# Selective scan of a vision mixer: two 512-column scans per state made one 1024-column scan, with the carried state added to the scan's input

## Chip, cores and metric

The kernel runs on one core of a Trainium2 chip. The metric is the device time in microseconds of the whole program, which computes a chain of network layers in one launch. The change touches the first layer only. Five engines work side by side: TensorE (PE, matmuls), VectorE (DVE), ScalarE (ACT), GpSimd (POOL) and SyncE (SP, which here only issues transfers). [...]

## The reference

The input is x of 2 x 64 x 64 x 128. Layer 0 normalises it, projects it to 256 channels, applies a depthwise 3 x 3 convolution and SiLU, and then runs a selective scan over the 4096 positions in four orders (K = 4: windows row by row, windows column by column, and both backwards). Cut to what matters:

```
delta = softplus(delta + delta_bias)
def step(h, inp):                      # h: 256 channels x 16 states, per order
    ut, dt, bt, ct = inp
    dA = exp(dt[..., None] * A4)       # A4 = -exp(A_logs)
    h = dA * h + (dt * ut)[..., None] * bt[:, :, None, :]
    y = einsum('bkdn,bkn->bkd', h, ct)
    return (h, y)
_, ys = lax.scan(step, zeros, xs_t)
y = ys + u * D
```

The four results are added, normalised over the channels, multiplied with SiLU(z) and projected back to 128 channels. Layers 1 (a deformable convolution), 2 (a larger selective scan and a spectral filter) and 3 (linear attention and experts) follow, each on the whole result of the one before.

## The kernel before

The 256 channels are two halves (h = 0, 1) of 128 partitions. For each of the two batch entries, and each of the four orders in the sequence kk = 0, 2, 1, 3, the 4096 positions are cut into eight **chunks** of T = 512 columns (ci = 0 to 7). Orders 2 and 3 run backwards: the access pattern of the scan is reversed, and the chunks come last to first. There are 2 x 4 x 8 = 64 chunks, and in each 16 **steps**, one for each state n.

A step does the following.

- POOL: S = du * B_n for both halves (L342, 1024 columns). du is dt times u, B_n a row spread over the partitions by a transfer into br. S has four buffers.
- ACT: dA = exp(dt * A_n) for each half (L345, 512 columns, in PSUM, four buffers of 512 columns).
- DVE: one scan for each half (L347), in place in S: S = dA * previous + S. Its initial value is 0 in the first chunk of an order and stt otherwise, the state kept from the chunk before.
- ACT: copies the last column of both halves into stt (L349), except in the last chunk.
- DVE: M = S * C_n for both halves (L361). C_n is spread over the partitions by a matmul into pcn (L316, one buffer).
- PE: adds M to yp through a multiplication by the identity (L376).

The section of steps is written under a manual schedule, so every engine's order is the order of the text. In each step the copy into stt is issued after the exponentials of that step but belongs to the step before. At step 0 the result of the chunk before is added into Y: by DVE for kk = 2 (L329) and for odd kk (L323), by a copy on ACT for kk = 0 (L327). Then u times D opens the new yp (L358).

The **prologue** of the next chunk (its u in scan order, the projections, softplus and du) is a generator, and each step of the current chunk advances it by one stage (`next(steps, None)`, behind M). Softplus is relu(v) + log(1 + e) with e = exp(-|v|), and the rounding of 1 + e is corrected by e - (u - 1), where u = 1 + e. By stage:

- 0 and 1: uc, the chunk's u, copied on ACT (L249, L253); 2: the projection px (PE, L257)
- 3: xd and its bf16 cast cs (ACT, L260, L265), xd's rows to DRAM, the matmul pd for half 0
- 4: r = xd - cs on POOL (L279), |v| and relu(v) of half 0 (ACT, L280, L281), pd for half 1; 5: |v| and relu(v) of half 1
- 6: two casts of r (ACT, L283, L284), e = exp (ACT, L285); 7: the third part of r (POOL, L287), u = 1 + e (ACT, L288)
- 8: dt += e (POOL, L290), a cast (ACT, L291), the logarithm into e (ACT, L292); it needs another function table, and the next dA needs the table of exp again
- 9: u - 1 (POOL, L294); 10: e - u (POOL, L296); 11: dt += e (POOL, L298); 12: du = dt * uc (POOL, L300)

Layer 2 of the same kernel, which the change leaves alone, already carries its state in the way that the change brings to layer 0: its scan starts from 0 in every chunk, and POOL multiplies the state by the first column's exponential (L1069) and adds it to the first column of S (L1070) behind the product that fills S (L1064).

Of the kernel before, what the change touches and what calls it, by code (L numbers as in the profile page):

```python
# [16 lines left out]
F32 = mybir.dt.float32  # L17
I32 = mybir.dt.int32
BF16 = mybir.dt.bfloat16
AF = mybir.ActivationFunctionType  # L20
ALU = mybir.AluOpType
AX = mybir.AxisListType
PSUM = bass.MemoryType.PSUM
DRAM = bass.MemoryType.DRAM

P = 128
# [132 lines left out]
def layer0(k):  # L159
    tc, nc, ins, X = k.tc, k.nc, k.ins, k.X  # L160
    T = N
    NC = L // T
    with ExitStack() as es:
# [18 lines left out]
        an = cst.tile([P, 8, 16], F32, name="an")  # L182
# [10 lines left out]
        for b in range(B):  # L193
# [36 lines left out]
            with ExitStack() as e2:  # L230
                ch = e2.enter_context(tc.tile_pool(name=f"l0h{b}", bufs=2))
# [2 lines left out]
                bcp = e2.enter_context(tc.tile_pool(name=f"l0e{b}", bufs=2, space=DRAM))  # L234
                ps = e2.enter_context(tc.tile_pool(name=f"l0ys{b}", bufs=1, space=PSUM))
                pc_ = e2.enter_context(tc.tile_pool(name=f"l0yc{b}", bufs=1, space=PSUM))
                pa = e2.enter_context(tc.tile_pool(name=f"l0ya{b}", bufs=4, space=PSUM))
                py = e2.enter_context(tc.tile_pool(name=f"l0yp{b}", bufs=1, space=PSUM))
                stt = sm.tile([P, 16, 2], F32, name="stt")

                def prologue(kk, c, got):


                    uc = ch.tile([P, 2, T], F32, name="uc")
                    for h in range(2):
                        if kk % 2:
                            src = U[:, h, :].rearrange("p (g i w j) -> p w g j i", g=4, i=16, w=4)[:, c // 2, 2 * (c % 2) : 2 * (c % 2) + 2]
                            for g in range(2):
                                nc.scalar.copy(uc[:, h, g * 256 : (g + 1) * 256].rearrange("p (j i) -> p j i", j=16), src[:, g])  # L249
                        else:  # L250
                            src = U[:, h, (c // 2) * 1024 : (c // 2 + 1) * 1024].rearrange("p (i w j) -> p w i j", i=16, w=4)
                            for g in range(2):
                                nc.scalar.copy(uc[:, h, g * 256 : (g + 1) * 256].rearrange("p (i j) -> p i j", i=16), src[:, 2 * (c % 2) + g])  # L253
                        yield
                    px = ps.tile([P, N], F32, name="pd", tag="ps")
                    for h in range(2):
                        nc.tensor.matmul(px, w_xp[:, h, kk, :], uc[:, h, :], start=h == 0, stop=h == 1)  # L257
                    yield
                    xd = ch.tile([P, T], F32, name="xd")
                    nc.scalar.copy(xd, px)  # L260
                    bc = bcp.tile([16, T], F32, name="bc")
                    nc.sync.dma_start(out=bc, in_=xd[112:128, :])

                    cs = ch.tile([80, T], BF16, name="cs")
                    nc.scalar.copy(cs, xd[:80])  # L265


                    dt = ch.tile([P, 2, T], F32, name="dt")
                    du = ch.tile([P, 2, T], F32, name="du")
                    e = sm.tile([P, 2, T], F32, name="e")  # L270
                    u = sm.tile([P, 2, T], F32, name="u")
                    for h in range(2):
                        bias = k.v("dt_b")[:, kk * 2 + h : kk * 2 + h + 1]
                        pd = ps.tile([P, N], F32, name="pd", tag="ps")
                        nc.tensor.matmul(pd, w_dt[96:104, kk, h * P : (h + 1) * P], xd[96:104, :], start=True, stop=True)
                        yield
                        if h == 0:
                            r = sm.tile([80, T], F32, name="r")
                            nc.gpsimd.tensor_tensor(r, xd[:80], cs, ALU.subtract)  # L279
                        nc.scalar.activation(e[:, h, :], pd, AF.Abs, bias=bias)  # L280
                        nc.scalar.activation(dt[:, h, :], pd, AF.Relu, bias=bias)  # L281
                    yield
                    nc.scalar.copy(cs[32:64], r[32:64])  # L283
                    nc.scalar.copy(cs[64:80], r[64:80])  # L284
                    nc.scalar.activation(e, e, AF.Exp, scale=-1.0)  # L285
                    yield
                    nc.gpsimd.tensor_tensor(r[64:80], r[64:80], cs[64:80], ALU.subtract)  # L287
                    nc.scalar.activation(u, e, AF.Identity, bias=1.0)  # L288
                    yield
                    nc.gpsimd.tensor_tensor(dt, dt, e, ALU.add)  # L290
                    nc.scalar.copy(cs[64:80], r[64:80])  # L291
                    nc.scalar.activation(e, u, AF.Ln)  # L292
                    yield
                    nc.gpsimd.tensor_scalar(u, u, -1.0, None, ALU.add)  # L294
                    yield
                    nc.gpsimd.tensor_tensor(e, e, u, ALU.subtract)  # L296
                    yield
                    nc.gpsimd.tensor_tensor(dt, dt, e, ALU.add)  # L298
                    yield
                    nc.gpsimd.tensor_tensor(du, dt, uc, ALU.mult)  # L300
                    got.append((uc, bc, cs, dt, du))

                todo = [(kk, ci) for kk in (0, 2, 1, 3) for ci in range(NC)]
                at = lambda i: (todo[i][0], NC - 1 - todo[i][1] if todo[i][0] >= 2 else todo[i][1])
                ready = []
# [25 lines left out]
                with tc.manual_schedule():  # L331
                    rows, pcn, last, save = spread(ready[0][1], 0), c_row(ready[0][2], 0), None, None
                    for it, (kk, ci) in enumerate(todo):
                        c = at(it)[1]
                        uc, bc, cs, dt, du = ready.pop()
                        steps = prologue(*at(it + 1), ready) if it + 1 < len(todo) else iter(())
                        s_ = slice(None, None, -1) if kk >= 2 else slice(None)
                        for n in range(16):
                            if n % 4 == 0:
                                br = rows  # L340
                            S = wk.tile([P, 2, T], F32, name="S", bufs=4)
                            nc.gpsimd.tensor_tensor(S, du, br[:, n % 4, :].unsqueeze(1).to_broadcast([P, 2, T]), ALU.mult)  # L342
                            for h in range(2):
                                dA = pa.tile([P, T], F32, name="dA")
                                nc.scalar.activation(dA, dt[:, h, :], AF.Exp, scale=an[:, kk * 2 + h, n : n + 1])  # L345
                                init = 0.0 if ci == 0 else stt[:, n, h : h + 1]
                                nc.vector.tensor_tensor_scan(S[:, h, s_], dA[:, s_], S[:, h, s_], init, ALU.mult, ALU.add)  # L347
                            if save is not None:
                                nc.scalar.copy(*save)  # L349
                                save = None  # L350
                            if ci < NC - 1:
                                save = stt[:, n, :], (S[:, :, 0] if kk >= 2 else S[:, :, T - 1])
                            if n == 0:
                                if last is not None:
                                    add_up(*last)
                                yp = py.tile([P, 2, T], F32, name="yp")
                                for h in range(2):
                                    nc.tensor.matmul(yp[:, h, :], dd[:, kk * 2 + h, :], uc[:, h, :], start=True, stop=False)  # L358
                                last = kk, c, yp
                            M = wk.tile([P, 2, T], F32, name="M")  # L360
                            nc.vector.tensor_tensor(M, S, pcn.unsqueeze(1).to_broadcast([P, 2, T]), ALU.mult)  # L361
                            next(steps, None)
                            if n == 14:
                                for _ in steps:
                                    pass
                            if n < 15:
                                pcn = c_row(cs, n + 1)
                            elif ready:
                                pcn = c_row(ready[0][2], 0)
                            if n % 4 == 2:  # L370
                                if n < 14:
                                    rows = spread(bc, n // 4 + 1)
                                elif ready:
                                    rows = spread(ready[0][1], 0)
                            for h in range(2):
                                nc.tensor.matmul(yp[:, h, :], k.ident, M[:, h, :], start=False, stop=n == 15)  # L376
                    add_up(*last)
# [1111 lines left out]
```

## Time and profile before

| what | value |
|---|---|
| median of 3 runs | 16227.84 us (16219.87 to 16235.26) |
| profiled execution: its own time, span | 16221.3 us, 16219.5 us |
| busy DVE, POOL, PE, ACT over the span | 13938.5, 13438.3, 12269.0, 9683.1 us |
| layer 0, first and last scan (L347) | start at 250.4 and 4630.4 us |
| POOL idle before r (L279), in 64 chunks | 798.2 us |
| ACT table loads at L292 and L345 | 64 of each, 1283 ns |
| POOL u - 1 (L294), ACT 1 + e (L288) | 2769 ns, 1051 ns |

The span runs from the first to the last instruction. Busy time of an engine over the whole span says little here: layer 2's scan (L1120, 8192 instructions) alone is 9225.0 us of DVE. What the change is worth has to be read between about 250 and 4630 us. In a row of the page, "us, ns" after the bar are the group's busy time and the mean of one instruction; then comes the idle time of the engine just before these instructions, and who ended it.

### The profile page before, as it was taken

What the parts mean: (1) busy time and instruction counts of PE and PEld (TensorE: products, weight loads), DVE (VectorE), ACT (ScalarE), POOL (GpSimd) and SP (SyncE); (2) the same over time, 40 slices, a digit from 0 to 9 for tenths busy, and PEclk for the clock granted to TensorE, in tenths of its full rate; (3) what the DMA queues carried; (4) which work ended last, traced back from release to release, by engine and by line L of the source; (5) the groups of instructions that cost most, each with busy time, mean ns of one, the idle gap of its engine ahead of it and who ended that gap; (6) DMA issues with size and microseconds to landing.
All of it is one profiled execution on the core that took longest, in us unless ns stands there. A gap on an engine that the chain in (4) does not pass through costs nothing.

```text
span 16219.5 us, 191958 instructions
## 1 busy us (share of the span) xinstructions
PE 12269.0 (76%) x69886; PEld 7241.8 (45%) x69886; DVE 13938.5 (86%) x13011; ACT 9683.1 (60%) x15720; POOL 13438.3 (83%) x4181
## 2 busy tenths in 40 slices
PE   6666657666657874548688688888888888888897
PEld 2222223222225861215455355555545555555565
DVE  4999985999974349999999999999999999999973
ACT  3555534555520017777777677777777777777752
POOL 3888744888735879999999999999999999999970
PEclk8999989999988886769899799999999999999998
DMA  2111111111125544546565555655666666665553
GB/s 101 68 68 66 66 48 52 68 68 66 66 73 162 161 146 151 164 153 198 180 195 193 171 187 192 195 190 196 189 199 195 192 204 196 188 205 195 187 173 128
DMA packets 1214866, 2389.74 MB, mean 147 GB/s; under 512 B 346648, under 2 KB 923288, under 8 KB 1047904
## 3 DMA queue, kind: packets, MB, share of 16 engines
q1 hardware_dynamic: 1162672, 2206.74, 41.5%
q0 software_dynamic: 50384, 169.42, 3.5%
q8 instruction: 552, 9.04, 0.2%
q14 instruction: 394, 3.23, 0.1%
q10 hardware_dynamic: 864, 1.32, 0.0%
HBM read 2018.49 MB, written 358.65 MB: 147 GB/s over the span
## 4 chain that ended last, share of the span: by engine, by line
POOL 39%; DVE 18%; PE 15%; issue 5%; ACT 3%; DMA 3%; another core or an unknown queue 1%; SPq 0%; POOLq 0%; DVEq 0%; ACTq 0%
POOL S L1064 33%; DVE S L1120 11%; PE pef L948 6%; DVE S L347 5%; POOL G L516 2%; PE Z L1082 2%; DMA row<-drow 2%; PE acc L921 2%; POOL S L342 2%; PE pv L535 1%; PE pw L747 1%; PE po L468 1%; POOL S L1070 1%; DVE M L361 1%
## 5 line engine op out<-in xcount | busy, mean ns | idle before, releaser
L1120 DVE TENSOR_TENSOR_SCAN S<-dA,S 128x512 f32<-128x512 f32 x8192 | 9225.0, 1200 | 391.1 <-ACT dA L1118 209.4
L1064 POOL TENSOR_TENSOR S<-row,g 128x4096 f32<-128x4096 f32 x1024 | 9102.1, 8896 | 251.8 <-DMA row<-drow 191.1
L1118 ACT ACTIVATE dA<-row,a_t 128x512 f32<-128x512 f32 x8192 | 5615.4, 692 | 2148.0 <-DVE S L1120 2111.3
L1082 PE MATMUL Z<-S,cv 128*32 128x256 f32 x32768 | 2503.1, 435 | 1481.5 <-ACT ze L1088 1225.6
L948 PE MATMUL pef<-hk,ur 128*128 128x256 f32 x14336 | 3515.4, 388 | 135.4 <-ACT e L928 119.9
L948 PEld LDWEIGHTS pef<-hk,ur 128*128 128x128 f32 x14336 | 2647.1, 191 | 1076.7 <-issue 565.5
L342 POOL TENSOR_TENSOR S<-du,br 128x1024 f32<-128x1024 f32 x1024 | 2389.7, 2355 | 204.8 <-issue 109.2
L347 DVE TENSOR_TENSOR_SCAN S<-dA,stt,S 128x512 f32<-128x512 f32 x1792 | 2198.3, 1268 | 127.7 <-POOL S L342 95.5
L1082 PEld LDWEIGHTS Z<-S,cv 128*32 128x32 f32 x32768 | 1000.8, 121 | 2690.6 <-issue 1283.4
L376 PE MATMUL yp<-M,ident 128*128 128x512 f32 x4096 | 2091.7, 635 | 3.2 <-DVE M L361 3.2
L376 PEld LDWEIGHTS yp<-M,ident 128*128 128x128 f32 x4096 | 821.5, 201 | 2180.2 <-issue 2141.7
L345 ACT ACTIVATE dA<-dt,an 128x512 f32<-128x512 f32 x2048 | 1332.3, 680 | 187.5 <-DVE S L347 173.3
L316 PE MATMUL pcn<-cs,sel 80*128 80x512 bf16 x1024 | 405.6, 396 | 1261.6 <-DVE M L361 1212.4
L361 DVE TENSOR_TENSOR M<-S,pcn 128x1024 f32<-128x1024 f32 x1024 | 1250.6, 1221 | 108.2 <-PE pcn L316 4.8
L1088 ACT COPY ze<-Z 128x512 f32<-128x512 f32 x1024 | 1122.9, 1097 | 234.1 <-PE Z L1082 200.2
L921 PE MATMUL acc<-e,mw 128*128 128x512 f32 x1920 | 1043.5, 631 | 31.7 <-ACT e L928 31.1
L516 POOL DMA_INDIRECT G<-table,idx x576 | 797.1, 1384 | 261.1 <-issue 175.1
L349 ACT COPY stt<-S 128x2 f32<-128x2 f32 x896 | 170.8, 191 | 1376.3 <-DVE S L347 1365.7
L948 PEld LDWEIGHTS pef<-hd,ur 128*128 128x128 f32 x4096 | 758.1, 194 | 493.9 <-issue 235.4
L948 PE MATMUL pef<-hd,ur 128*128 128x256 f32 (+1 forms) x4096 | 876.7, 340 | 103.2 <-ACT e L928 97.2
L523 DVE TENSOR_TENSOR V<-G,wt 128x4608 f32<-128x4608 f32 x64 | 317.6, 4962 | 603.3 <-DMA G<-table,idx 594.8
L279 POOL TENSOR_TENSOR r<-xd,cs 80x512 f32<-80x512 f32 x64 | 73.8, 1152 | 798.2 <-ACT cs L265 798.2
(319 smaller groups left out, 9010.1 us busy)
## 6 DMA issues: line engine op xcount, KB each, us to landing
row<-drow SPq DMA_DIRECT2D x1024, 1024.0 KB
br<-bc SPq DMA_DIRECT2D x256, 1024.0 KB
zd<-ze SPq DMA_DIRECT2D x1024, 256.0 KB
hk<-in_phi_dram SPq DMA_DIRECT2D x128, 576.5 KB
hk<-in_phi_dram SPq DMA_DIRECT2D x96, 704.5 KB
hd<-in_phi_dram SPq DMA_DIRECT2D x512, 128.5 KB
mw<-wdr SPq DMA_DIRECT2D x480, 128.0 KB
hk<-in_phi_dram SPq DMA_DIRECT2D x160, 320.5 KB
```

What stands on the lines that cost most here:

```text
L342: nc.gpsimd.tensor_tensor(S, du, br[:, n % 4, :].unsqueeze(1).to_broadcast([P, 2, T]), ALU.mult)
L345: nc.scalar.activation(dA, dt[:, h, :], AF.Exp, scale=an[:, kk * 2 + h, n : n + 1])
L347: nc.vector.tensor_tensor_scan(S[:, h, s_], dA[:, s_], S[:, h, s_], init, ALU.mult, ALU.add)
L361: nc.vector.tensor_tensor(M, S, pcn.unsqueeze(1).to_broadcast([P, 2, T]), ALU.mult)
L376: nc.tensor.matmul(yp[:, h, :], k.ident, M[:, h, :], start=False, stop=n == 15)
L921: nc.tensor.matmul(acc.rearrange("p a s -> p (a s)"), ms[f][:, o, :], e, start=box["first"], stop="whole" in box and (f, o) == todo[-1])
L948: nc.tensor.matmul(pe[:, a, 256 - n :], ur[:, par, j, :], h[:, at : at + n], start=i == 0, stop=i + 1 == len(mm))
L1064: nc.gpsimd.tensor_tensor(S, row.unsqueeze(1).to_broadcast([P, 2, R, T]), g.unsqueeze(2).to_broadcast([P, 2, R, T]), ALU.mult)
L1082: nc.tensor.matmul(Z[32 * j : 32 * j + 32, q], cv[:, h, s], S[:, h, :, s], start=h == 0, stop=h == 1)
L1088: nc.scalar.copy(ze.rearrange("p q t e -> p q e t"), Z)
L1118: nc.scalar.activation(dA, row[:, j % R, :], AF.Exp, scale=a_t[:, h, d : d + 1])
L1120: nc.vector.tensor_tensor_scan(s, dA, s, 0.0, ALU.mult, ALU.add)
```

## The change

The two scans of a step become one over 2 x 512 columns, half 0 behind half 1 or the other way round, with initial value 0 throughout. So that one half doesn't run into the other, the exponential of each half's first column in scan order (f: column 0, or 511 backwards) is 0 in dA, set once for each order, and ACT writes only the other 511 columns. What the initial value did is now added to the input: POOL multiplies the kept state by ea, the exponential at column f for all 16 states, and adds it to column f of S. dA becomes two fixed buffers of 2 x 512 columns in place of four of 512. ea is computed by ACT at the end of the prologue. In the prologue u - 1 moves from POOL to ACT, and r is issued one stage later, at 5 in place of 4.

```
-  pa = ... tile_pool(name=f"l0ya{b}", bufs=4, space=PSUM)
+  pa = ... tile_pool(name=f"l0ya{b}", bufs=1, space=PSUM)
+  dAs = [pa.tile([P, 2, T], F32, name=f"dA{i}") for i in range(2)]
...
-                        if h == 0:
+                        if h == 1:
                             r = sm.tile([80, T], F32, name="r")
...
-                    nc.gpsimd.tensor_scalar(u, u, -1.0, None, ALU.add)
+                    nc.scalar.activation(u, u, AF.Identity, bias=-1.0)
...
-                    got.append((uc, bc, cs, dt, du))
+                    ea = ch.tile([P, 16, 2], F32, name="ea")
+                    f = T - 1 if kk >= 2 else 0
+                    for h in range(2):
+                        nc.scalar.activation(ea[:, :, h], an[:, kk * 2 + h, :], AF.Exp, scale=dt[:, h, f : f + 1])
+                    got.append((uc, bc, cs, dt, du, ea))
...
-                        uc, bc, cs, dt, du = ready.pop()
+                        uc, bc, cs, dt, du, ea = ready.pop()
+                        f = T - 1 if kk >= 2 else 0
+                        rest = slice(0, T - 1) if kk >= 2 else slice(1, T)
+                        if ci == 0:
+                            for t in dAs:
+                                nc.vector.memset(t[:, :, f : f + 1], 0.0)
...
                             nc.gpsimd.tensor_tensor(S, du, br[:, n % 4, :]..., ALU.mult)
+                            if ci > 0:
+                                if n in (0, 2):
+                                    m = slice(0, 14) if n == 0 else slice(14, 16)
+                                    nc.gpsimd.tensor_tensor(stt[:, m], stt[:, m], ea[:, m], ALU.mult)
+                                nc.gpsimd.tensor_tensor(S[:, :, f], S[:, :, f], stt[:, n, :], ALU.add)
+                            dA = dAs[n % 2]
                             for h in range(2):
-                                dA = pa.tile([P, T], F32, name="dA")
-                                nc.scalar.activation(dA, dt[:, h, :], AF.Exp, scale=an[:, kk * 2 + h, n : n + 1])
-                                init = 0.0 if ci == 0 else stt[:, n, h : h + 1]
-                                nc.vector.tensor_tensor_scan(S[:, h, s_], dA[:, s_], S[:, h, s_], init, ALU.mult, ALU.add)
+                                nc.scalar.activation(dA[:, h, rest], dt[:, h, rest], AF.Exp, scale=an[:, kk * 2 + h, n : n + 1])
+                            flat, dflat = (t.rearrange("p h t -> p (h t)")[:, s_] for t in (S, dA))
+                            nc.vector.tensor_tensor_scan(flat, dflat, flat, 0.0, ALU.mult, ALU.add)
```

More of the change, by code (lines that the diff above doesn't have):

```diff
@@ L236, in layer0 @@
                 pc_ = e2.enter_context(tc.tile_pool(name=f"l0yc{b}", bufs=1, space=PSUM))
-                pa = e2.enter_context(tc.tile_pool(name=f"l0ya{b}", bufs=4, space=PSUM))
+                pa = e2.enter_context(tc.tile_pool(name=f"l0ya{b}", bufs=1, space=PSUM))
                 py = e2.enter_context(tc.tile_pool(name=f"l0yp{b}", bufs=1, space=PSUM))
                 stt = sm.tile([P, 16, 2], F32, name="stt")
+                dAs = [pa.tile([P, 2, T], F32, name=f"dA{i}") for i in range(2)]
                 def prologue(kk, c, got):
```

## The prediction

> **What bounds the kernel now.** I read the busy times by stretch first, to see which engine is full while layer 0 runs; then the costliest groups, for the durations; then the timeline of one chunk, instruction by instruction, because a mean hides where the engines wait for each other. The table of stretches (after the length: busy and count of PE, PEld, DVE, ACT, POOL; then clock, DMA share, GB/s):
>
> ```profile
> 800.00:1200.00 400.00, 268.36 (x590) 104.88 (x589) 376.10 (x321) 217.08 (x414) 324.39 (x145) 0.94 0.18 66
> ```
>
> VectorE (DVE) is busy 376 of 400 us. GpSimd (POOL) has 324, so only about a fifth is spare there, and ScalarE (ACT) 217. From the page's costliest groups (the last bracket is idle time before the group and who ended it):
>
> ```profile
> L342 POOL TENSOR_TENSOR S<-du,br 128x1024 f32<-128x1024 f32 x1024 | 2389.7, 2355 | 204.8 <-issue 109.2
> L347 DVE TENSOR_TENSOR_SCAN S<-dA,stt,S 128x512 f32<-128x512 f32 x1792 | 2198.3, 1268 | 127.7 <-POOL S L342 95.5
> L345 ACT ACTIVATE dA<-dt,an 128x512 f32<-128x512 f32 x2048 | 1332.3, 680 | 187.5 <-DVE S L347 173.3
> L361 DVE TENSOR_TENSOR M<-S,pcn 128x1024 f32<-128x1024 f32 x1024 | 1250.6, 1221 | 108.2 <-PE pcn L316 4.8
> ```
>
> One chunk of the timeline (start, length, engine, line; a chunk has steps n = 0 to 15, and the first line is the scan pair of n = 7):
>
> ```profile
> 1025.97 2.45 DVE L347 TENSOR_TENSOR_SCAN S<-dA,stt,S 128x512 f32<-128x512 f32 x2
> ...
> 1028.51 0.20 ACT L349 COPY stt<-S 128x2 f32<-128x2 f32 x1 [1.35 <-DVE S L347]
> 1028.52 1.22 DVE L361 TENSOR_TENSOR M<-S,pcn 128x1024 f32<-128x1024 f32 x1
> ...
> 1029.36 1.28 ACT L292 ACT_TABLE_LOAD   x1
> 1029.66 2.45 DVE L347 TENSOR_TENSOR_SCAN S<-dA,stt,S 128x512 f32<-128x512 f32 x2
> ...
> 1031.73 1.28 ACT L345 ACT_TABLE_LOAD   x1
> 1031.80 2.77 POOL L294 TENSOR_SCALAR u<-u 128x1024 f32<-128x1024 f32 x1 [0.87 <-ACT e L292]
> ...
> 1033.02 1.30 ACT L345 ACTIVATE dA<-dt,an 128x512 f32<-128x512 f32 x2
> ...
> 1033.82 2.46 DVE L347 TENSOR_TENSOR_SCAN S<-dA,stt,S 128x512 f32<-128x512 f32 x2 [0.38 <-ACT dA L345]
> ...
> 1046.15 2.46 DVE L347 TENSOR_TENSOR_SCAN S<-dA,stt,S 128x512 f32<-128x512 f32 x2 [0.83 <-POOL S L342]
> ...
> 1048.38 16.21 POOL L342 TENSOR_TENSOR S<-du,br 128x1024 f32<-128x1024 f32 x7
> ...
> 1050.76 2.46 DVE L347 TENSOR_TENSOR_SCAN S<-dA,stt,S 128x512 f32<-128x512 f32 x2 [0.83 <-POOL S L342]
> ```
>
> A plain step takes 3.69 us (1025.97 to 1029.66): scan pair 2.45, a gap of 0.10 until M may read S, 1.14 to the next scan. The next chunk's L294 starts at 1094.53, so this chunk lasts 62.73 us. It has **two parts**. Part A runs from the end of scan 7 (E7, 1028.42) to the start of scan 13 (1050.76), 22.34 us, and is not set by VectorE: ACT's chain (state copy, cast, two table loads, Ln) releases L294 at 1031.80; from there POOL alternates S and softplus steps back to back (L294, S10, L296, S11, L298, S12, L300, S13) until scan 13. Part B, the other 40.39 us, is 11 scans and their M at VectorE's own pace. A faster scan pays only in B.
>
> [...]the trace has 1208 (initial value a constant) and 1268 (read from stt)[...] layer 2 prices it for a tiny add:
>
> ```profile
> 8999.16 8.87 POOL L1064 TENSOR_TENSOR S<-row,g 128x4096 f32<-128x4096 f32 x1
> 9008.11 0.21 POOL L1070 TENSOR_TENSOR S<-S,state 128x8 f32<-128x8 f32 x1
> 9008.26 8.87 POOL L1064 TENSOR_TENSOR S<-row,g 128x4096 f32<-128x4096 f32 x1
> ```
>
> Its add starts 0.08 after S ends and the next S 0.15 later.
>
> **The change part by part.**
> - Scan: 2048 of 512 columns become 1024 of 1024. [...] A step becomes 2.27 + 0.10 + 1.14 = 3.51 us, 0.188 less; 0.06 less where the initial value was a constant (pair 2.33). No trace shows a VectorE read across two PSUM banks, so bounds: [...]2.42 (2 x 1208, nothing shared).
> - State add on POOL: 896 instructions. S to the next instruction is 2.355 + 0.08 + 0.15 = 2.58 us instead of 2.31 (16.21 / 7): +0.27. Two elements instead of eight; bounds +0.15 to +0.35.
> - stt times ea, 112 on POOL at 0.25 (layer 2's L1069, 32 columns: 253 ns), and their waits for the copies of steps 13 and 15. Behind them are the new chunk's S0 and S2. S0 is ready 3 x 2.58 + 0.35 = 8.1 us after S13, its scan comes 3 x 3.51 = 10.5 after scan 13: counted at nothing.
> - u - 1 (64 x 2.77) leaves POOL; ACT gets 64 x 1.05 (price of L288, same operation and shape). It now stands behind the exp table load and the dA pair of step 9. The instruction order of the changed kernel shows no further table load. The two ea activations at step 12 (about 0.21 each, priced by L830's tiny Exp) have 3 us of slack before dA is due.
> - dA: a pair of halves is now one buffer, with two buffers as deep in steps as before. The scan waits for both halves, and the instruction order shows the second half waiting for the first: 0.68 + 0.06 + 0.68 = 1.42 until ready instead of 0.68.
> - r goes one step later: POOL's wait for it (1006.36 to 1012.79 here) is partly filled with S5. It is before part A: nothing.
> - Memsets of dA's reset column, 16 on VectorE at 0.15 (tiny VectorE rows take 0.15 to 0.16): 2.4 us.
> - No DMA is added or removed. SP's queue and PE's order hold the same instructions; PE has 268 of 400 us.
>
> **Part A after**, from E7: copy starts 0.09; to dA's start the same chain as now, 1033.02 - 1028.51 = 4.51; dA pair 1.42; state copy 0.05; u - 1 1.05; release 0.08: e - u (L296 now) starts at 7.20. POOL then: e - u 2.31, S11 2.58, dt 2.31, S12 2.58, du 2.31, S13 with its add 2.65, release 0.04. Sum 21.98 us, against 22.34: **only 0.36 less**. Moving u - 1 takes 2.77 off POOL and S10 in front of the wait, but puts ACT's table load, dA pair and 1.05 into the chain, and three adds come on top. POOL reaches that wait 1.2 us early, so the earlier adds cost nothing: L287 starts 1.68 after E5 (1022.71 against 1021.03), that is at E7 - 5.33; then 1.23, S8 2.58, L290 2.31, S9 and S10 5.17 end at 5.96.
>
> **Part B after**: ten steps at 0.188 and the last scan at 0.18: 2.06 less. Where kk = 2 the chunk saves 0.36 + 2.06 = 2.42. Where kk is odd, M of step 1 waits for PE's pcn (0.35 to 0.51 at 1510.86 and 1574.94); PE's chain stays, so 0.2 is lost: 2.2. Where kk = 0, scan 1 waits for ACT, which copies Y after PE's last matmuls (0.88 idle at 629.74). dA's second half adds 0.74 and the shorter first scan 0.18; 0.9 is lost: 1.5. A first chunk (ci = 0) has no adds, but init-0 scans and memsets: 1.5. A last chunk without prologue is pure VectorE: 3.0.
>
> Sum: 14 x 1.5 + 14 x 2.42 + 26 x 2.2 + 2 x 3.0 + 8 x 1.5 = 130 us. Layer 1 waits for all of layer 0, so this reaches the end. From the profiled execution (span 16219.5, its own time 16221.3, 6.5 below the median) that is a span of 16089.5 and a time of 16091; from the median, **16098 us**.
>
> **Rivals.**
> - *Two PSUM banks cost two fixed parts*: scan 2.42, so B gets 11 x 0.15 x 64 = 105 us back: 16203, no change. For it: no row shows such a read. [...]
> - *POOL becomes the bound* (slower). If the two-element add with its 2 KB stride, or the wait for S to land, cost 1.0 us instead of 0.27, part A gains 3 x 0.73 and the S in front of it (8 to 10) another 3 x 0.73 less the 1.2 of slack: 3.2 us per chunk, 56 x 3.2 = 179, so 16277. It decides from about 0.86 per add, where 6 extra adds less 1.2 come to 130 / 56. Against: 896 adds of layer 2 with the same kind of stride lie between 199 and 227 ns.
> - *Part A gives way*: if u - 1 reached POOL without delay, VectorE would set all 16 steps: A = 1.24 + 5 x 3.51 = 18.8, 3.2 x 64 = 205 more, 15893. Against: the two table loads stand in the trace.
> - That the change doesn't do what it says: the instruction order shows 1024-column scans, so no.
>
> **How the numbers follow.** About 0.2% (32 us) is what a measurement of this kernel can tell from no change. Main case 0.83; two banks 0.10, partly still inside faster; POOL 0.05; A gives way 0.02. Faster 0.86, same 0.08, slower 0.06. [...]the adds' upper bound 3 x 0.08 x 56 = 13 more. The range 16030 to 16185 takes most of these and stops short of the full two-bank case.
>
> **What would show it.** Right: one scan row of 1024 columns near 2270 ns x1024; steps of 3.51 us; scan 9 idle about 1.3 us on ACT's dA (0.38 now); scans 12 and 13 still ended by POOL; chunk 60.3 us where kk = 2; r's wait on POOL much smaller than 798 us; POOL's add near 210 ns. Wrong: a scan over 2.4 us, an add over 0.5 us, scan 9 without a wait, or a chunk below 59 or above 62 us.

## The result, and the profile after

The changed kernel takes 16122.86 us (median of 4 runs, 16111.22 to 16126.88) against 16227.4 us (4 runs, 16219.87 to 16235.26): a ratio of 0.9933, 95% interval 0.9921 to 0.9944, or 104.5 us less. The forecast was 16098 us, 130 less. The profiled execution took 16122.4 us, its span 16120.6.

First the stretch that answers to the one shown of before (length; busy and count of PE, PEld, DVE, ACT, POOL; clock, DMA share, GB/s):

```profile
800.00:1200.00 400.00, 275.52 (x615) 109.17 (x615) 372.91 (x227) 249.48 (x452) 342.36 (x264) 0.96 0.19 69
```

VectorE is as full as it was, with 227 instructions in place of 321. ScalarE went from 217 to 249 us and GpSimd from 324 to 342 in the same stretch, and that stretch now holds more steps. Nothing has become idle; the work moves through faster. The same groups on the page (busy time and mean, then idle time ahead):

```profile
L365 DVE TENSOR_TENSOR_SCAN S<-dA,S 128x1024 f32<-128x1024 f32 x1024 | 2339.1, 2284 | 243.7 <-ACT dA L363 96.8
L354 POOL TENSOR_TENSOR S<-du,br 128x1024 f32<-128x1024 f32 x1024 | 2410.3, 2357 | 138.6 <-DVE M L379 83.3
L363 ACT ACTIVATE dA<-dt,an 128x511 f32<-128x511 f32 x2048 | 1406.9, 687 | 209.0 <-DVE S L365 132.0
L379 DVE TENSOR_TENSOR M<-S,pcn 128x1024 f32<-128x1024 f32 x1024 | 1250.5, 1221 | 110.5 <-DVE S L365 6.9
```

One scan of 1024 columns takes 2284 ns where the pair took 2450 to 2460; M is unchanged. The page names ACT's dA as what ended the largest share of the scan's idle time (96.8 of 243.7 us), but POOL comes under two lines. VectorE's table of waits in layer 0 has both (total, times, longest):

```profile
DVE S L365 <- ACT dA L363: 96.8, 78, 2.4
...
DVE S L365 <- POOL S L360: 82.4, 100, 1.3
...
DVE S L365 <- POOL S L354: 56.7, 10, 25.5
```

L360 is the new state add, L354 is S itself (two of its ten waits, of 25.5 us each, are the starts of the two batch entries). The new small instruction on POOL, and the two waits for r, from the groups of POOL within layer 0:

```profile
L360 POOL TENSOR_TENSOR S<-S,stt 128x2 f32<-128x2 f32 x896 | 173.8, 194 | 65.9
...
L289 POOL TENSOR_TENSOR r<-r,cs 16x512 f32<-16x512 f32 x64 | 73.9, 1154 | 181.4 <-ACT cs L286 181.4
L281 POOL TENSOR_TENSOR r<-xd,cs 80x512 f32<-80x512 f32 x63 | 72.7, 1154 | 336.4 <-ACT cs L267 336.4
```

And part A of the chunk with kk = 2, from the timeline (start, length, engine, line; the first line is scan 7, the last is scan 13):

```profile
1005.31 2.28 DVE L365 TENSOR_TENSOR_SCAN S<-dA,S 128x1024 f32<-128x1024 f32 x1
...
1012.13 1.41 ACT L363 ACTIVATE dA<-dt,an 128x511 f32<-128x511 f32 x2
...
1013.56 1.05 ACT L296 ACTIVATE u<-u 128x1024 f32<-128x1024 f32 x1
1013.64 2.29 DVE L365 TENSOR_TENSOR_SCAN S<-dA,S 128x1024 f32<-128x1024 f32 x1 [1.20 <-ACT dA L363]
...
1014.69 2.35 POOL L298 TENSOR_TENSOR e<-e,u 128x1024 f32<-128x1024 f32 x1 [1.20 <-ACT u L296]
...
1024.56 2.29 DVE L365 TENSOR_TENSOR_SCAN S<-dA,S 128x1024 f32<-128x1024 f32 x1 [0.25 <-POOL S L360]
...
1029.45 2.29 DVE L365 TENSOR_TENSOR_SCAN S<-dA,S 128x1024 f32<-128x1024 f32 x1 [1.27 <-POOL S L360]
```

Scan 7 ends at 1007.59 and scan 13 starts at 1029.45: part A lasts 21.86 us. Scan 9 waits 1.20 us for the pair of exponentials, POOL waits 1.20 us for ACT's u - 1, and POOL still ends the waits of scans 12 and 13.

The last addition into X at the end of layer 0 starts at 4788.2 us before and at 4672.9 after: **layer 0 gained 115.3 us** in these two executions, and the layers behind it, which are the same code, took longer in the one after (11431.3 us from there to the end of the span before, 11447.7 after). The changed kernel and the four below that should end layer 0 with it give 4665.4 to 4675.1, so a few microseconds between two executions say little.

### The profile page after: what moved, and what is told of

It reads as the page before. It is cut to its first block, busy times and chain, and to the rows that moved or that the text cites. A ratio compares the mean times of both kernels' runs of the same rounds, so it can differ in the third digit from the quotient of the medians.

```text
span 16120.6 us, 190989 instructions
## 1 busy us (share of the span) xinstructions
PE 12236.8 (76%) x69886; PEld 7246.4 (45%) x69886; DVE 13783.2 (86%) x12003; ACT 9835.0 (61%) x15912; POOL 13463.0 (84%) x5125
## 4 chain that ended last, share of the span: by engine, by line
POOL 34%; PE 13%; DVE 10%; DMA 3%; ACT 2%; issue 1%; SPq 0%; POOLq 0%; ACTq 0%; DVEq 0%
POOL S L1082 33%; DVE S L1138 10%; PE pef L966 6%; PE Z L1100 2%; PE acc L939 2%; DMA row<-drow 2%; PE pw L765 1%; POOL S L1088 1%; ACT ze L1106 1%; ACT dA L1136 0%; DMA w<-in_w_b_dram 0%; DMA w<-in_w_delta_dram 0%; ACT e L946 0%; PE acc L1001 0%; DMA e<-mdr 0%
## 5 line engine op out<-in xcount | busy, mean ns | idle before, releaser
L365 DVE TENSOR_TENSOR_SCAN S<-dA,S 128x1024 f32<-128x1024 f32 x1024 | 2339.1, 2284 | 243.7 <-ACT dA L363 96.8
L354 POOL TENSOR_TENSOR S<-du,br 128x1024 f32<-128x1024 f32 x1024 | 2410.3, 2357 | 138.6 <-DVE M L379 83.3
L363 ACT ACTIVATE dA<-dt,an 128x511 f32<-128x511 f32 x2048 | 1406.9, 687 | 209.0 <-DVE S L365 132.0
L966 PE MATMUL pef<-hd,ur 128*128 128x256 f32 (+1 forms) x4096 | 882.0, 342 | 99.8 <-ACT e L946 93.8
L553 PE MATMUL pv<-ident,V 128*128 128x128 f32 x4608 | 615.3, 302 | 52.1 <-issue 48.8
```

Of the source, the lines that this page charges most:

```text
L363: nc.scalar.activation(dA[:, h, rest], dt[:, h, rest], AF.Exp, scale=an[:, kk * 2 + h, n : n + 1])
L365: nc.vector.tensor_tensor_scan(flat, dflat, flat, 0.0, ALU.mult, ALU.add)
L966: nc.tensor.matmul(pe[:, a, 256 - n :], ur[:, par, j, :], h[:, at : at + n], start=i == 0, stop=i + 1 == len(mm))
```

## Experiments

My theory was the prediction's: a chunk is a part A, paced by ACT's chain and POOL's queue, and a part B at VectorE's pace; the merged scan pays in B alone, and the move of u - 1 is what keeps A from growing. Against it stood that VectorE's time is the whole story (u - 1 and the adds hidden), and that the chunk follows ACT or POOL throughout. "Layer 0 ends" below means the start of the last addition into X.

### The merged scan without the move of u - 1

On top of the changed kernel:

```
-                    nc.scalar.activation(u, u, AF.Identity, bias=-1.0)
+                    nc.gpsimd.tensor_scalar(u, u, -1.0, None, ALU.add)
```

> The changed kernel with u - 1 back on GpSimd. My theory: a chunk is part A (end of scan 7 to start of scan 13, set by ScalarE's table loads and then GpSimd) and part B (11 scans at VectorE's pace), and without the move part A is 3.33 + 2.73 + 2.58 + 2.31 + 2.58 + 2.31 + 2.58 + 2.31 + 2.69 = 23.4 us in place of 21.86: 62 chunks x 1.56 = 97 us slower than the changed kernel, 16220, so that the merged scan alone gains almost nothing over the kernel before. Rival (VectorE sets every step, the merged scan pays 16 times in a chunk whatever GpSimd does): about 16123, as the changed kernel.

Measured: 16227.94 us against 16232.79 before, ratio 0.9997 (0.9989 to 1.0005). Scans 7, 12 and 13 of one chunk in its timeline, and u - 1 on POOL:

```profile
1024.61 2.28 DVE L365 TENSOR_TENSOR_SCAN S<-dA,S 128x1024 f32<-128x1024 f32 x1
...
1030.21 2.77 POOL L296 TENSOR_SCALAR u<-u 128x1024 f32<-128x1024 f32 x1
...
1045.36 2.29 DVE L365 TENSOR_TENSOR_SCAN S<-dA,S 128x1024 f32<-128x1024 f32 x1 [1.26 <-POOL S L360]
1050.24 2.29 DVE L365 TENSOR_TENSOR_SCAN S<-dA,S 128x1024 f32<-128x1024 f32 x1 [1.26 <-POOL S L360]
```

Part A is 23.35 us (1026.89 to 1050.24), 1.01 longer than before the change: from u - 1 to scan 13 four state adds have joined POOL's queue (4 x 0.27 = 1.1 us by the prediction's price) and nothing has left it. Layer 0 ends at 4776.7, only 11.5 earlier than before. The merged scan alone is worth nothing that can be measured in the whole program.

### The move of u - 1 without the merged scan

On the kernel before, the opposite edit:

```
-                    nc.gpsimd.tensor_scalar(u, u, -1.0, None, ALU.add)
+                    nc.scalar.activation(u, u, AF.Identity, bias=-1.0)
```

> The kernel before with one edit, u - 1 on ScalarE in place of GpSimd; two 512-column scans as before, no state adds. My theory: part A falls from 22.34 to 7.07 + 5 x 2.31 + 2.40 = 21.0 us, 62 x 1.3 = 82 us, so 16145: most of the change's gain without the merged scan. Rival (the gain is the scan's): no change, 16227.

Measured: 16152.48 us, ratio 0.9953 (0.994 to 0.9967). Scan pair 7, e - u on POOL, scan pair 13:

```profile
1007.89 2.45 DVE L347 TENSOR_TENSOR_SCAN S<-dA,stt,S 128x512 f32<-128x512 f32 x2
...
1017.40 2.35 POOL L296 TENSOR_TENSOR e<-e,u 128x1024 f32<-128x1024 f32 x1 [2.23 <-ACT u L294]
...
1031.35 2.46 DVE L347 TENSOR_TENSOR_SCAN S<-dA,stt,S 128x512 f32<-128x512 f32 x2 [0.74 <-POOL S L342]
```

Part A is 21.01 us (1010.34 to 1031.35), 1.33 shorter, and layer 0 ends at 4703.6, 84.6 earlier: 1.33 x 62 = 82. One line of the diff thus brings most of the gain. With the merged scan in place it is worth more, 4776.7 - 4672.9 = 103.8; in turn the merged scan, worth 11.5 alone, adds 4703.6 - 4672.9 = 30.7 us to the move.

### An idle memset in part B and in part A

To see where VectorE's own time counts, an extra memset into a tile that nobody reads was put behind four scans, in steps 1 to 4 (B) or 9 to 12 (A). First with 256 columns:

```
                             nc.vector.tensor_tensor_scan(flat, dflat, flat, 0.0, ALU.mult, ALU.add)
+                            if n in (1, 2, 3, 4):           # or (9, 10, 11, 12)
+                                nc.vector.memset(idle, 0.0) # 128 x 256
```

> The same extra memsets behind the scans of steps 1, 2, 3 and 4, in part B. Both theories: 64 x 0.8 = 51 us slower than the changed kernel, 16174; it is the measure for the run with the memsets in part A.

> The changed kernel with an extra VectorE memset of 128 x 256 into a scratch tile behind the scans of steps 9, 10, 11 and 12 (about 0.27 us each, 0.2 of it beyond the gap ahead of M). My theory: these steps lie in part A, where scans 12 and 13 wait 1.7 us for GpSimd, so 4 x 0.2 = 0.8 us per chunk disappears: 16123, within 10. Rival (VectorE's own time is the bound in every step): 64 x 0.8 = 51 us slower, 16174.

Measured: 16124.24 us (0.9936, 0.9922 to 0.9949) and 16114.15 us (0.993, 0.9916 to 0.9943). The first missed its number by 50 us, and the pair tells nothing on A and B, for the probe cost nothing anywhere. The timeline of a step of the first kernel:

```profile
1045.76 2.28 DVE L366 TENSOR_TENSOR_SCAN S<-dA,S 128x1024 f32<-128x1024 f32 x1
1048.04 0.27 DVE L368 MEMSET idle<- 128x256 f32 x1
1048.23 1.16 DVE L382 TENSOR_TENSOR M<-S,pcn 128x1024 f32<-128x1024 f32 x1
1049.31 2.28 DVE L366 TENSOR_TENSOR_SCAN S<-dA,S 128x1024 f32<-128x1024 f32 x1
```

The step takes 3.55 us, 0.02 more than without the memset of 0.27. M starts 0.19 us behind the scan's end, where in a plain step it starts 0.10 behind it, and then takes 1.16 in place of 1.22: 0.09 later and 0.06 shorter. So 0.25 of the memset's 0.27 us do not show; why is open. The first of the next two texts takes 0.25 us for the gap between a scan and its M, but it is the hidden share: the gap in the timeline is 0.10. The pair was repeated with 512 columns (the same edit, `idle` of 128 x 512).

> The changed kernel with an extra VectorE memset of 128x512 into a tile that nobody reads, behind the scans of steps 1 to 4 (part B). The memset of 256 columns lay in the 0.25 us or so between a scan and its M and cost 0.02 us; one of 512 columns should take about 0.54 us and stick out of that gap by about 0.29. My theory (part B is VectorE's pace, so what VectorE gains or loses there is the kernel's): 4 x 0.29 x 64 = 74 us, less some 10 where M of step 1 waits for PE anyway in the 32 chunks with odd kk: 16123 + 65 = 16188, layer 0 ends near 4738. Rival (the whole chunk follows ACT or POOL, VectorE's time is hidden everywhere): 16123, no change. A second rival (the memset costs its full length here): 4 x 0.54 x 64 = 138, 16261.

> The same extra memset of 512 columns behind the scans of steps 9 to 12 (part A). VectorE stands idle 0.25 + 1.27 us ahead of scans 12 and 13 there, waiting for POOL, and four memsets that stick out by 0.29 make 1.16: my theory says that POOL still ends scan 13's wait and nothing changes, 16115 to 16125, layer 0 ends near 4670. Rival (VectorE sets the pace of all 16 steps): the same 65 to 74 us slower as at steps 1 to 4, 16188.

Measured: in B 16198.18 us (0.9978, 0.997 to 0.9986), in A 16130.76 us (0.9935, 0.9922 to 0.9949, the ratio of the changed kernel itself). Layer 0 ends at 4747.3 and 4675.1. Timeline of the first, a padded step in B:

```profile
999.00 2.28 DVE L366 TENSOR_TENSOR_SCAN S<-dA,S 128x1024 f32<-128x1024 f32 x1
1001.34 0.48 DVE L368 MEMSET idle<- 128x512 f32 x1
1001.74 1.16 DVE L382 TENSOR_TENSOR M<-S,pcn 128x1024 f32<-128x1024 f32 x1
1002.82 2.28 DVE L366 TENSOR_TENSOR_SCAN S<-dA,S 128x1024 f32<-128x1024 f32 x1
```

and scans 9 and 13 of the second, padded in A:

```profile
1014.51 2.29 DVE L366 TENSOR_TENSOR_SCAN S<-dA,S 128x1024 f32<-128x1024 f32 x1 [1.20 <-ACT dA L364]
...
1030.32 2.29 DVE L366 TENSOR_TENSOR_SCAN S<-dA,S 128x1024 f32<-128x1024 f32 x1 [0.46 <-POOL S L361]
```

A padded step takes 3.82 us, 0.29 more. In B that is 4 x 0.29 x 64 = 74 us, and layer 0 ends 74.4 later than in the changed kernel. (That the two agree to half a microsecond is luck: a chunk in the middle of an order grew by 1.1 to 1.6 us, depending on kk, and the 10 us that were taken off for odd kk did not show.) In A the same 74 us of VectorE's time vanish: the four memsets use up the 0.25 us of waiting ahead of scan 12 and 0.81 of the 1.27 ahead of scan 13, and POOL still ends the wait for scan 13. Part B is VectorE's, part A is not.

### More room between the prologue's stages

If POOL's row of prologue steps and S sets part A, then one S more between those steps should shorten it. Two more stages are left empty, so that dt comes at 12 and du at 14:

```
                     nc.gpsimd.tensor_tensor(e, e, u, ALU.subtract)
                     yield
+                    yield
                     nc.gpsimd.tensor_tensor(dt, dt, e, ALU.add)
                     yield
+                    yield
                     nc.gpsimd.tensor_tensor(du, dt, uc, ALU.mult)
```

> The changed kernel with two more pauses in the prologue: the second dt += e is issued at step 12 in place of 11, du and ea at 14 in place of 12, so that GpSimd fills two S between them. My theory: S is then never late, scans 12 and 13 stop waiting, part A falls to 6.05 + 4 x 3.53 = 20.2 us: 62 x 1.7 = 105 us faster than the changed kernel, 16018. Rival (GpSimd is the bound over the whole chunk, 54 us of work and its waits): the lateness comes back at later scans, 16123 or a little less.

Measured: 16027.51 us, ratio 0.9873 (0.9858 to 0.9889); layer 0 ends at 4576.7, 96 before the changed kernel. Scan 9 of two successive chunks in the timeline, and two rows of VectorE's table of waits in layer 0 (total, times, longest):

```profile
992.43 2.29 DVE L367 TENSOR_TENSOR_SCAN S<-dA,S 128x1024 f32<-128x1024 f32 x1 [1.20 <-ACT dA L365]
...
1051.21 2.29 DVE L367 TENSOR_TENSOR_SCAN S<-dA,S 128x1024 f32<-128x1024 f32 x1 [1.20 <-ACT dA L365]
```

```profile
DVE S L367 <- ACT dA L365: 90.1, 73, 1.8
...
DVE S L367 <- POOL S L362: 10.0, 8, 1.6
```

The chunk takes 58.78 us, part A 20.15. The waits for POOL's state add were 82.4 us in the changed kernel and are 10.0 here; those for ACT's exponentials were 96.8 and are 90.1. With POOL out of the way, the wait that is left in part A is scan 9's for ACT's exponentials, behind the cast, the logarithm and the two table loads of stages 8 and 9 (0.61, 1.06 and twice 1.28 us in the changed kernel's timeline).

### The reset column set earlier

At the start of an order VectorE clears the reset column of both dA buffers. In the changed kernel, at the first change of order:

```profile
736.47 1.22 DVE L379 TENSOR_TENSOR M<-S,pcn 128x1024 f32<-128x1024 f32 x1
737.70 0.06 DVE L347 MEMSET dA<- 128x2 f32 x2
737.79 1.41 ACT L363 ACTIVATE dA<-dt,an 128x511 f32<-128x511 f32 x2 [7.03 <-DVE dA L347]
739.29 2.29 DVE L365 TENSOR_TENSOR_SCAN S<-dA,S 128x1024 f32<-128x1024 f32 x1 [1.53 <-ACT dA L363]
```

The memset takes 0.06 us, but it stands behind M of step 15, ACT waits 7.03 us for it, and then scan 0 waits for ACT. The experiment sets the column of the next order right behind a buffer's last scan:

```
-                        if ci == 0:
+                        if it == 0:
...
+                            if ci == NC - 1 and n >= 14 and it + 1 < len(todo):
+                                g = T - 1 if todo[it + 1][0] >= 2 else 0
+                                nc.vector.memset(dA[:, :, g : g + 1], 0.0)
```

> The changed kernel with the reset column of each dA buffer written right behind that buffer's last scan of an order (steps 14 and 15) in place of ahead of the next order's first step. My theory: ScalarE's exponentials for the new order stop waiting for VectorE's memset (42 us over 6 waits now), the first scan of orders 2, 1 and 3 starts 1.5 us earlier, 4 to 6 places with about 2 us each: 6 to 12 us less. Rival (the wait is hidden): nothing.

One execution: layer 0 ends at 4662.4, 10.5 earlier. Scan 0 of the new order, at 737.00, follows M without a wait:

```profile
732.42 1.22 DVE L382 TENSOR_TENSOR M<-S,pcn 128x1024 f32<-128x1024 f32 x1
732.45 0.06 DVE L368 MEMSET dA<- 128x2 f32 x1
732.54 1.42 ACT L363 ACTIVATE dA<-dt,an 128x511 f32<-128x511 f32 x2 [2.25 <-DVE dA L368]
```

```profile
735.90 0.06 DVE L368 MEMSET dA<- 128x2 f32 x1
737.00 2.28 DVE L365 TENSOR_TENSOR_SCAN S<-dA,S 128x1024 f32<-128x1024 f32 x1
...
742.39 2.29 DVE L365 TENSOR_TENSOR_SCAN S<-dA,S 128x1024 f32<-128x1024 f32 x1 [1.77 <-ACT dA L363]
```

At this change, to order 2, most of the wait only moves to scan 1 (the last line), which needs ACT behind its copy of Y; in the kernel before, scan 1 waits there too (1.0 and 1.3 us). In the changed kernel scan 0 waits 1.53 us at each of the six changes of order, and here at none. From scan 0 of an order's last chunk to scan 0 of the next order's second chunk, the early reset saves 0.7 us at the two changes to order 2, 1.8 and 2.1 at those to order 1, and 2.4 at both to order 3: 10.1 together. In the three other kernels that leave these steps as in the changed one (r back, memsets of 256 in A, of 512 in A), the same six places together differ from it by -1.9 to +0.7 us.

The whole program took 16122.58 us all the same, since the other layers took 10.7 us more in this execution. So the wait and about 10 us in layer 0 are shown; a shorter program is not, by this run.

### r back at stage 4

```
-                        if h == 1:
+                        if h == 0:
                             r = sm.tile([80, T], F32, name="r")
```

> The changed kernel with r issued at step 4 again. My theory: r, S5, S6 and S7 end before the casts of step 6 release L289, so the chunk keeps its 60.5 us (kk = 2) and the time is unchanged, 16123 within 10; only the place of GpSimd's wait moves. Rival (the later r is part of the gain): slower by up to 64 x 1.15 = 74 us.

One execution: 16115.35 us, and layer 0 ends at 4668.6 (4672.9 with r at 5). POOL then waits 555 us for r and 25 for its third part, in place of 336 and 181 in the lines above. The wait changes place, and layer 0 keeps its length within the scatter given above.

### The three together

More room, the early reset, and the last cast of r (`nc.scalar.copy(cs[64:80], r[64:80])`, ahead of the logarithm at stage 8) moved to stage 10, out of ACT's chain:

```
-                    nc.scalar.copy(cs[64:80], r[64:80])
                     nc.scalar.activation(e, u, AF.Ln)
                     yield
                     nc.scalar.activation(u, u, AF.Identity, bias=-1.0)
                     yield
+                    nc.scalar.copy(cs[64:80], r[64:80])
```

> The changed kernel with the two more pauses, the early reset, and the last cast of r (0.62 us) moved from step 8, ahead of the logarithm, to step 10. My theory: with GpSimd out of the way only ScalarE's chain ends part A's waits, so the cast's 0.63 us comes off scan 9's wait (1.20 left, 0.6 after): 62 x 0.63 = 39 us, and about 10 for the reset, from 16028: 15979. Rival (scan 9's wait is not the cast's): 16018.

Measured: 15984.74 us (15979.2 to 15986.94), ratio 0.985 (0.9835 to 0.9865). Layer 0 ends at 4529.2, 143.7 before the changed kernel, and scan 9's wait has shrunk:

```profile
985.47 2.29 DVE L367 TENSOR_TENSOR_SCAN S<-dA,S 128x1024 f32<-128x1024 f32 x1 [0.55 <-ACT dA L365]
...
1043.60 2.29 DVE L367 TENSOR_TENSOR_SCAN S<-dA,S 128x1024 f32<-128x1024 f32 x1 [0.55 <-ACT dA L365]
```

A chunk is 58.13 us: 16 steps of 3.525, about 1.2 for adding Y, and 0.55 of waiting. This version beats both kernels. What is left of such a chunk is nearly all scan and M.

## Why the prediction was right, and where it was off

| step of the prediction | forecast | measured |
|---|---|---|
| scan of 1024 columns | 2267 ns | 2284 ns |
| plain step | 3.51 us | 3.525 us |
| state add; S to the next S | near 210 ns; 2.58 us | 194 ns; 2.58 us |
| dA pair; u - 1 on ACT | 1.42; 1.05 us | 1.41; 1.05 us |
| scan 9's wait for dA | 1.3 us | 1.20 us |
| part A (kk = 2) | 21.98 us | 21.86 us |
| chunk with kk = 2 | 60.3 us | 60.49 us |
| gain per chunk inside an order: kk = 0, kk = 2, odd kk | 1.5, 2.42, 2.2 us | 1.34, 2.30, 2.20 us (means of 12, 12, 24 chunks) |
| these 48 chunks | 99.8 us | 96.5 us |
| first chunks of orders (8), last chunks before a change of order (6) | 24.2 us | 12.8 us |
| the two chunks without a prologue | 6.0 us | 3.8 us |

Chunks are measured from scan 0 to scan 0. They gained 113.1 us together; of the other 2.2, 1.2 is an earlier first scan.

**The split into A and B held, and it is the cause.** The means over the 48 chunks inside an order, from the timelines (part A from the end of scan 7 to the start of scan 13, part B the rest):

| kernel | part A | part B |
|---|---|---|
| before | 22.35 us | 41.06 us |
| merged scan alone | 23.37 | 39.57 |
| move of u - 1 alone | 21.01 | 41.06 |
| both (the changed kernel) | 21.85 | 39.56 |
| and memsets of 512 in B | 21.85 | 40.84 |
| and memsets of 512 in A | 21.85 | 39.56 |
| and more room for POOL | 20.20 | 39.56 |

The merged scan shortens B by 1.5 us whatever A does, and lengthens A by 0.8 to 1.0. The move of u - 1, more room for POOL and memsets in A leave B alone; memsets in B leave A alone. The step's saving (3.69 - 3.525) over all 16 steps would have given 0.165 x 16 x 64 = 169 us, and the merge alone gave nothing.

**The scan** was mis-sized by 17 ns: 11 x 0.017 x 64 = 12 us of the 15 that layer 0 fell short. The 2267 ns were an assumption that no trace of the kernel before shows: all its scans have 512 columns (1200 ns in layer 2, 1208 and 1268 in layer 0), so they don't tell what a longer one takes. With both lengths measured, the second 512 columns cost 2284 - 1208 = 1076 ns, and an estimate from these two numbers, if the time grows evenly with the columns, leaves 1208 - 1076 = 132 ns that don't depend on them. The rival of two fixed parts (2 x 1208 ns, 2.42 us) is out: the scan takes 2284.

The title's part of this saving is the smaller one. A pair with a constant start takes 2.33 us, as in the first chunks of the kernel before, and one that reads its start from stt 2.45: of the 0.17 us that the new scan saves, 0.12 comes from the constant start, which the state add makes possible, and 0.05 from one scan in place of two. No run has two scans with a constant start and the state add; it would leave most of the saving in B, by this reckoning.

**Part A** came out 0.12 us shorter than the sum, 62 x 0.12 = 7 us in favour, an error that hides part of the others: e - u started at E7 + 7.10 (1014.69 - 1007.59), where 7.20 was worked out.

**The memsets** were the step that failed. They were priced at 16 x 0.15 = 2.4 us of VectorE. Their own time is 0.06 us for two; what counts is that ACT waits for them, behind M of step 15, before it may fill dA for the new order. The prediction asked only what the memset costs on its engine, and not who waits for it: scan 0 stands idle 1.53 us at each of the six changes of order, and the early reset brought about 10 us back. 12 - 7 + 10 = 15 is the shortfall of layer 0 (115.3 against 130). By chunks it lies where it should: of it, 11.4 us are missing in the chunks on the two sides of a change of order and at the starts, 3.3 in the 48 inside an order, and 2.2 in the two without a prologue, less 2.2 that lie outside the chunks.

**r** was rightly priced at nothing, and its wait did fall (from 577 and 100 us for the two waits within layer 0 to 336 and 181), though by less than "much smaller" promised.

**POOL as the bound by the adds** is out: an add lengthens POOL's queue by 2.58 - 2.31 = 0.27 us, far from 0.86. **Part A gives way** did not come true in this kernel. The table loads (twice 1.28 us) were only part of the reason: of the 3 us between 21.85 and the 18.8 of that rival, more room for POOL took 1.65, and scan 9's wait for ACT is 1.20, half of which went with the cast. (The rival's 205 us also counted 64 chunks, where 62 have a prologue.)

**What stays open** is the stretch behind layer 0. From layer 0's last addition to the end of the span, the kernel before took 11431 us, the least of the twelve profiled executions, the one after 11448, and the ten experiments 11437 to 11461. No instruction there was edited. Some 6 us of it come with the merged scan: from L1185 of the kernel before, in layer 3, to the last addition into X, all ten kernels with the merged scan take 6.0 to 7.2 us longer than the kernel before, and the move of u - 1 alone 0.2 less. The difference arises in the experts' matmuls, where TensorE was granted a lower clock. Here are 95 us of them, before and after (columns as in the table of stretches, the clock third from the end):

```profile
16110.90:16205.90 95.00, 75.27 (x861) 51.40 (x861) 14.15 (x30) 9.32 (x21) 2.10 (x3) 0.84 0.72 291
```

```profile
16006.00:16101.00 95.00, 74.19 (x801) 48.92 (x800) 9.46 (x22) 9.33 (x21) 2.10 (x3) 0.77 0.68 279
```

The clock in this stretch is 0.77 in all ten kernels with the merged scan and 0.84 in the two without. Why a change in layer 0 goes with a lower clock in layer 3 no run shows. The rest differs from run to run: the stretch of layer 2's scans took from 3 us less to 14 us more than in the kernel before.

## What to carry to other kernels

Before a cheaper instruction is priced by its count, cut the loop into the stretches that its engine paces and those that another's queue paces, and count it in the first only; here 5 of 16 steps paid nothing. Where a change puts small instructions on a second engine, see whether something can be taken off that engine in the same stretch: here the one-line move was worth more than the rewrite (84.6 us against 11.5, each alone). For every small initialisation ask who waits for it and behind what it stands: 0.06 us of memset cost a 1.53 us stall at each of six places.

## What the hardware showed that I had not expected

- An independent memset on VectorE between a scan and the M that reads its result cost less than its own length: 0.27 us of memset lengthened the step by 0.02, 0.48 us by 0.29.
- A scan of 1024 columns took 2284 ns, 132 less than twice the 1208 of 512 columns with a constant start. With its initial value read from stt a scan of 512 columns took 60 ns more (1268 against 1208).
- On POOL an addition took 194 ns on 2 columns, a multiplication 203 on 4 and 247 on 28. The idle time ahead of the state add, which needs the S just before it, adds 0.07 each (65.9 us over 896).
- The same matmuls of layer 3 were granted a TensorE clock of 0.77 with the merged scan in layer 0 and 0.84 without it (95 us of the profiled executions, twelve kernels); why is open.
